# Seven of eight chunk pairs by Strassen's form, statistics by ScalarE's squares, and T1/T4 products one stage later, in a two-layer interaction kernel

## The chip, the cores and the metric

The kernel runs on one core of a Trainium2 chip. The metric is the device time of one execution in microseconds; a time quoted here is the median of the runs of its kernel, three to twenty-three of them. All profiles shown are of runs in the fast state, at a granted TensorE clock of 0.99 to 1.00.

## The reference

Two layers. Each forms all products of the fields of its input with the 32 fields of x, contracts them with a weight matrix, and normalizes each output channel over all rows and embedding places. Half of the first layer's output feeds the second.

```
def _batchnorm(h, gamma, beta):          # h: [4096, 128, 16]
    mean, var over (rows, embedding)
    return (h - mean) * rsqrt(var + 1e-5) * gamma + beta
def _cin_layer(out, x, W, b, gamma, beta):
    h = einsum('rne,rfe->rnfe', out, x).reshape(r, -1, e)
    h = einsum('rce,oc->roe', h, W) + b
    return _batchnorm(h, gamma, beta)
h1 = _cin_layer(x, x, W1, ...)           # W1: [128, 1024]
out, direct1 = h1[:, :64], h1[:, 64:]
direct2 = _cin_layer(out, x, W2, ...)    # W2: [128, 2048]
return concatenate([direct1, direct2], axis=1).sum(axis=-1)
```

## The kernel before

The change is in the second layer. It goes through 64 chunks; a chunk holds two groups of 512 sites. In each chunk there are four stages (i = 3, 0, 1, 2), and in each stage two slices q of 128 contraction rows. One stage and one slice make a product of 2 x 2 blocks: two halves of 64 output channels, two operands. Done plainly it needs eight products of 128x64 weights with 128x512 data; in Strassen's form (Winograd's variant) it needs seven, with sums of weight blocks S1 to S4, made once, and sums of data T1 to T4. T3 comes out of VectorE's multiply directly, because the difference of the x fields is multiplied; GpSimd adds T2 = T3 + B11 and then in one instruction T1 and T4 (B22 - T2 and B21 - T2). Eight such "pairs" of stage and slice make a chunk. Before the change six of them are Strassen's (stages S1, S2, S3) and two plain (stage P, i = 3), so 6 x 7 + 2 x 8 = 58 products.

A product has 64 output columns and uses one half of TensorE's columns ("low" or "high" by its place in the PSUM bank); two products on different halves run together (in the trace of the kernel before they start 0.01 us apart, and the next two 0.43 us later). Products are named x0 to x7 by the accumulator that they add to; a bank holds two accumulators (bank x62 has x6 low and x2 high). In the changed code `x1`, `x32`, `x67` and `x54` issue a stage's products for these accumulators; `x54` are those of T1 and T4.

```
STAGES = (3, 0, 1, 2); PLAIN = 3
psum  = tile_pool(name="psum", bufs=6, PSUM); factors = tile_pool(bufs=2, PSUM)
z2pool = tile_pool(name="z2pool", bufs=3); tpool = tile_pool(name="tpool", bufs=2)

def strassen(sums_, i, z, stop):
    t = tpool.tile([P, 3, 2, T], FP, tag="t", name="t")
    b11, t3, b22, b21 = (z[:, k] for k in range(4))
    t2, t1, t4 = (t[:, k] for k in range(3))
    queue("pool", lambda: nc.gpsimd.tensor_tensor(t2, t3, b11, ALU.add))
    twice = t2.unsqueeze(1).to_broadcast([P, 2, 2, T])
    queue("pool", lambda: nc.gpsimd.tensor_tensor(t[:, 1:3], z[:, 2:4], twice, ALU.subtract))
    sums_.matmul(1, w[0][0], b11[:, 0], stop)
    sums_.matmul(0, w[1][0], b11[:, 1], stop)
    for (x, kx, bx), (y, ky, by) in (
        ((3, 7, b22), (2, 2, b21)), ((6, 5, t2), (7, 6, t3)), ((5, 4, t1), (4, 3, t4)),
    ):
        for q in range(2): ...        # one product on each half

# combine(c): nine steps, spread over the next chunk:
#   both (ScalarE, from bank x11), both + x11, e = both + x62, u2, u3 = u2 + x57, ...,
#   statistics of e (VectorE), sums over embedding (VectorE)
```

VectorE writes z by two multiplies a stage, the factors f come from ScalarE, and `combine` finishes the chunk before, between them. The program gives every engine its instructions in a fixed order. A tile of t, of which there are two buffers, takes the buffer of the tile two before it, and its first writer waits for the last reader of that whole tile: in the changed kernel S2's T2 sum starts 0.09 us after the end of P's last T4 product, which had read another part of it (the timelines in the result).

## Time and profile before

| | before |
|---|---|
| time | 2125.4 us |
| second layer | from 501 us to the end |
| products in it | 64 x 58, two passes each of 0.429 us |
| once-a-chunk interval, mean of the last 62 | 25.02 us |

The lines, and the busy time of each engine in the second layer, are in the prediction. The once-a-chunk interval is that between the starts of the ScalarE instruction `both<-x`; I leave out the first interval, as the pipeline fills there.

### The profile page before, as it was taken

To read this page: it belongs to the slowest core of one execution; us is meant where nothing else is said; L and a number is where in the kernel's file an instruction comes from. 1 tells how busy PE (TensorE), PEld (TensorE's weight loads), DVE (VectorE), ACT (ScalarE), POOL (GpSimd) and SP (SyncE) were. 2 spreads that over 40 slices of the span, in tenths; PEclk is the share of its full clock that TensorE was granted. 3 is DMA by queue.
4 is the path that set the end of the run, shared out by engine and by line. 5 is a ranking of instruction groups with operands and counts; after the bars stand their busy time and mean duration, and the time that the engine had idled before them with its cause. 6 is when DMAs were issued, how large, how long until landed. Compare 5 with 4: busy or idle time off the path is not lost.

```text
span 2125.5 us, 23438 instructions
## 1 busy us (share of the span) xinstructions
PE 2095.5 (99%) x8732; PEld 736.3 (35%) x8732; DVE 1911.2 (90%) x1461; ACT 856.5 (40%) x1236; POOL 1330.4 (63%) x391
## 2 busy tenths in 40 slices
PE   9999999999999999999999999999999999999996
PEld 3444444443333333333333333333333333333332
DVE  7988879887999999899999998999999989999996
ACT  3555555553443333333333333333333333433332
POOL 0000000003888888878888888788888888888885
PEclk9999999999999999999999999999999999999998
DMA  9999999997677777776668777766677777676751
GB/s 348 359 341 345 326 342 365 364 334 201 159 168 189 181 183 172 172 174 159 165 162 198 173 172 173 174 161 166 162 179 171 171 174 172 164 166 161 171 137 40
DMA packets 112019, 440.65 MB, mean 207 GB/s; under 512 B 13088, under 2 KB 13088, under 8 KB 103456
## 3 DMA queue, kind: packets, MB, share of 16 engines
q1 hardware_dynamic: 105456, 418.43, 72.9%
q10 hardware_dynamic: 6448, 20.72, 2.6%
q8 instruction: 68, 1.11, 0.2%
q14 instruction: 47, 0.39, 0.1%
HBM read 417.07 MB, written 22.02 MB: 207 GB/s over the span
## 4 chain that ended last, share of the span: by engine, by line
PE 85%; POOL 9%; DVE 3%; issue 2%; ACT 1%; DMA 0%; DVEq 0%; SPq 0%; POOLq 0%
PE x L521 62%; PE ps L378 21%; POOL t L540 6%; POOL t L537 3%; PE ps L340 2%; DVE zz L491 2%; ACT both L483 1%; DMA b<-in_xb 0%; DVE e L486 0%; DVE zz L496 0%; PE running L404 0%; DVE x L188 0%; DVE z L347 0%; DVE d L687 0%; ACT u L483 0%
## 5 line engine op out<-in xcount | busy, mean ns | idle before, releaser
L521 PE MATMUL x<-zz,w_sb 128*64 128x512 f32 x2560 | 966.0, 592 | 0.0
L521 PE MATMUL x<-zz,s_sb 128*64 128x512 f32 x2048 | 932.4, 592 | 0.7 <-PE running L404 0.7
L537 POOL TENSOR_TENSOR t<-zz 128x1024 f32<-128x1024 f32 x192 | 456.6, 2378 | 753.0 <-DVE zz L491 753.0
L540 POOL TENSOR_TENSOR t<-zz,t 128x2048 f32<-128x2048 f32 x192 | 876.0, 4562 | 15.0
L521 PE MATMUL x<-t,s_sb 128*64 128x512 f32 x1536 | 696.1, 594 | 6.8 <-POOL t L540 6.4
L483 ACT ACTIVATE f<-a,keep 128x512 f32<-128x512 f32 x512 | 398.2, 778 | 629.9 <-DVE zz L491 623.8
L491 DVE TENSOR_TENSOR zz<-f,b 128x2048 f32<-128x2048 f32 x255 | 580.5, 2277 | 0.0
L491 DVE TENSOR_TENSOR zz<-f,bx 128x2048 f32<-128x2048 f32 x255 | 580.5, 2276 | 0.0
L378 PE MATMUL ps<-z,w_sb 128*128 128x512 f32 x1024 | 450.4, 597 | 2.2 <-DVE z L347 2.2
L521 PEld LDWEIGHTS x<-zz,s_sb 128*64 128x64 f32 x2048 | 280.5, 137 | 366.1 <-issue 350.3
L521 PEld LDWEIGHTS x<-t,s_sb 128*64 128x64 f32 x1536 | 205.2, 137 | 456.7 <-issue 396.7
L521 PE MATMUL x<-t,w_sb 128*64 128x512 f32 x768 | 363.2, 595 | 0.0
L347 DVE TENSOR_TENSOR z<-a,b 128x2048 f32<-128x2048 f32 (+1 forms) x129 | 293.6, 2277 | 62.8 <-DMA b<-in_xb 35.9
L521 PEld LDWEIGHTS x<-zz,w_sb 128*64 128x64 f32 x2560 | 300.6, 137 | 109.6 <-issue 106.1
L378 PEld LDWEIGHTS ps<-z,w_sb 128*128 128x128 f32 x1024 | 192.2, 190 | 258.0 <-issue 246.0
L521 PE MATMUL x<-zz,neg_sb 128*64 128x512 f32 x512 | 240.6, 592 | 0.0
L305 ACT ACTIVATE e<-ps,bn_sb 128x512 f32<-128x512 f32 x127 | 87.2, 687 | 240.9 <-PE ps L378 206.7
L486 DVE TENSOR_TENSOR both<-both,x 128x512 f32<-128x512 f32 x64 | 44.0, 688 | 130.2 <-ACT both L483 130.2
L483 ACT ACTIVATE u<-e,bn_sb 64x512 f32<-64x512 f32 x64 | 46.2, 722 | 193.6 <-DVE e L486 193.6
L521 PEld LDWEIGHTS x<-zz,neg_sb 128*64 128x64 f32 x512 | 70.1, 137 | 145.9 <-issue 145.9
L521 PEld LDWEIGHTS x<-t,w_sb 128*64 128x64 f32 x768 | 100.0, 137 | 0.0
L483 ACT ACTIVATE both<-x 64x512 f32<-64x512 f32 x64 | 38.0, 593 | 138.7 <-PE x L521 138.7
(74 smaller groups left out, 894.4 us busy)
## 6 DMA issues: line engine op xcount, KB each, us to landing
a<-h SPq DMA_DIRECT2D x256, 512.0 KB, 5.4
a<-in_xa SPq DMA_DIRECT2D x128, 512.0 KB, 6.0
b<-in_xb SPq DMA_DIRECT2D x128, 512.0 KB, 7.0
b<-in_xb SPq DMA_DIRECT2D x64, 1024.0 KB, 7.1
bx<-in_xb SPq DMA_DIRECT2D x64, 512.0 KB, 6.1
bx<-x SPq DMA_DIRECT2D x64, 512.0 KB, 7.9
h<-kept ACTq DMA_DIRECT2D x64, 256.0 KB, 5.8
r<-in_xr SPq DMA_DIRECT2D x16, 512.0 KB, 8.2
```

The source lines that it names most:

```text
L305: nc.scalar.activation(e, ps, AF.Identity, bias=b1)
L340: nc.tensor.matmul(pss[t + k], w1_sb[rows, 4 + t % GROUP // 4, :], zr[rows, :], start=not ended, stop=ended)
L347: return nc.vector.tensor_tensor(z[:, k], a.rearrange("p (a t) -> p a t", a=2)[:, k].unsqueeze(2).to_broadcast([P, n, 2, T]), b.rearrange( ...
L378: nc.tensor.matmul(pss[t], w1_sb[:, m, :], z[:, m // 2, m % 2, :], start=(t == m == 0), stop=(t > 0 and m == 3))
L483: return queue("act", lambda: nc.scalar.activation(to, source, AF.Identity, **scale_bias))
L486: return dve(lambda: nc.vector.tensor_tensor(to, x, y, ALU.add))
L491: dve(lambda: nc.vector.tensor_tensor(z, a, b.rearrange("p (k q) t -> p k q t", k=2), ALU.mult))
L521: queue("pe", lambda: nc.tensor.matmul(self.of[x], w, b, start=start, stop=stop))
L537: queue("pool", lambda: nc.gpsimd.tensor_tensor(t2, t3, b11, ALU.add))
L540: queue("pool", lambda: nc.gpsimd.tensor_tensor(t[:, 1:3], z[:, 2:4], twice, ALU.subtract))
```

## The change

Three things, meant to take work off TensorE and VectorE. First, one slice of the plain stage goes to Strassen's form too: 57 products a chunk; since that is odd, the half on which a chunk begins alternates, so that two chunks fill both halves evenly. Second, VectorE's statistics of the second layer go to ScalarE as squares with an accumulated sum (except in the last two chunks), and the difference of two x tiles becomes a reduction with a single operand, after ScalarE has negated one of them. Third, the products of T1 and T4, which wait for GpSimd longest (in the kernel before, TensorE's products and weight loads wait 65.8 us in all for T1/T4 sums and 0.4 us for T2 sums), are issued one stage later.

```diff
+            self.qs = (1,) if i == PLAIN else (0, 1)
+            t = tpool.tile([P, 3, 2, T], FP, tag="t", name="t")
+            ...
+            q = slice(self.qs[0], 2)
+            n = len(self.qs)
+            queue("pool", lambda: nc.gpsimd.tensor_tensor(t[:, 0, q], z[:, 1, q], z[:, 0, q], ALU.add))
+            twice = t[:, 0, q].unsqueeze(1).to_broadcast([P, 2, n, T])
+            queue("pool", lambda: nc.gpsimd.tensor_tensor(t[:, 1:3, q], z[:, 2:4, q], twice, ALU.subtract))
 ...
-        dve(lambda: stats_x.add(e[:, 0]))
-        dve(lambda: stats_y.add(e[:, 1]))
+        if c < MOST:
+            queue("act", lambda: add_square(c, 0, e))
 ...
-                ordinary(sums_, z)
+                stage.ordinary(low_first, 0)
+                stage.x1(low_first)
             else:
-                strassen(sums_, i, z, k == 3)
+                stage.x1(not low_first)
+            stage.x32(not low_first)
+            if k > 0:
+                waiting.x54(not low_first)
+            stage.x67(not low_first)
+            waiting = stage
+            if k == 3:
+                stage.x54(not low_first)
```

(Cut: the statistics' totals on ScalarE, the difference, and the order of PSUM banks, x11 now first.)

More of the change, by code (lines that the diff above doesn't have):

```diff
@@ L175, in load_bx, with negate @@
         return bx
-    xs = {}
+    xs = xpool.tile([P, 2, 2 * T], FP, tag="x", name="xs")
+    xd = xpool.tile([P, 2 * T], FP, tag="xd", name="xd")
     def load_x(g, k):
-        x = xs[k] = xpool.tile([P, 2 * T], FP, tag=f"x{k}", name="x")
         at = xb.offset + ((2 * DIFF * g + 1) * WRAP + 2 * k) * T
-        nc.sync.dma_start(x, bass.AP(xb.tensor, at, [[2 * WRAP * T, DIFF], [4 * T, 8], [1, 2 * T]]))
+        nc.sync.dma_start(xs[:, k], bass.AP(xb.tensor, at, [[2 * WRAP * T, DIFF], [4 * T, 8], [1, 2 * T]]))
+    def negate(part):
+        x = xs[:, 0, part * T : (part + 1) * T]
+        return nc.scalar.activation(x, x, AF.Identity, scale=-1.0)
     def difference(part):
-        cols = slice(part * T // 2, (part + 1) * T // 2)
-        return nc.vector.tensor_tensor(xs[1][:, cols], xs[1][:, cols], xs[0][:, cols], ALU.subtract)
+        to = slice(part * T // 2, (part + 1) * T // 2)
+        return nc.vector.tensor_reduce(xd[:, to], xs[:, :, to].rearrange("p k t -> p t k"), AX.X, ALU.add)
     def store_difference(g):
-        return nc.scalar.dma_start(diffs[g], xs[1])
+        return nc.scalar.dma_start(diffs[g], xd)
     EARLY = [(12, lambda: load_x(0, 1)), (16, lambda: load_x(0, 0)), (41, lambda: store_difference(0))]
+    EARLY += [(30 + 2 * k, lambda k=k: negate(k)) for k in range(2)]
     EARLY += [(34 + 2 * k, lambda k=k: difference(k)) for k in range(4)]
@@ L314, in finish @@
                 return ps
-            evict_direct(ed[to, :], ps)
+            done = evict_direct(ed[to, :], ps)
             if half == 1:
                 sum_direct(c)
+            return done
         def evict_direct(ed, ps):
-            nc.scalar.activation(ed, ps[KEEP:, :], AF.Identity, bias=b1[KEEP:])
+            return nc.scalar.activation(ed, ps[KEEP:, :], AF.Identity, bias=b1[KEEP:])
         def sum_direct(c):
@@ L383, in tile_cin @@
             if t > 0:
-                finish(t - 1)
+                evicted = finish(t - 1)
             if t == 20:
                 combine_weights()
-            with tc.issue_after(loads[-1].ins), tc.issue_after(product.ins):
+            if t == 0:
+                continue
+            with tc.issue_after(loads[-1].ins), tc.issue_after(product.ins), tc.issue_after(evicted.ins):
                 if t == 12:
@@ L453, in tile_cin @@
     d2 = sums.tile([P, 2, NC, RT], FP, tag="sum2", name="d2")
-    groups_of = -(-(NC - LAST) // SG) + 1
-    groups2 = const.tile([P, 2, groups_of, 3], FP, tag="groups2", name="groups2")
-    stats_x, stats_y = Stats("x", NC), Stats("y", NC, groups2[:, 0])
-    for g, size in enumerate(stats_x.sizes):
-        nc.vector.memset(groups2[:, 1, g, 0:1], size / LAST)
-    def swap_group(g):
+    MOST = NC - 2
+    groups_x = const.tile([P, 5, 3], FP, tag="groupsx", name="groups_x")
+    groups2 = const.tile([P, 2, 5, 3], FP, tag="groups2", name="groups2")
@@ new lines, in tile_cin @@
+    for group in (groups_x, groups2[:, 0]):
+        nc.vector.memset(group[:, 0, 0:1], float(MOST * T))
+    groups_of = (groups_x, groups2[:, 0])
+    squares = const.tile([P, 2, MOST], FP, tag="squares", name="squares")
+    totals = const.tile([P, 2, 4], FP, tag="totals", name="totals")
+    first = const.tile([P, 2, 6], FP, tag="first", name="first")
+    center = const.tile([P, 2, 1], FP, tag="center", name="center")
+    moments = const.tile([P, 2, 4], FP, tag="moments", name="moments")
@@ new lines, in tile_cin, with find_center, add_square, sum_up @@
+    unread = cpool.tile([P, T], FP, tag="unread", name="unread")
+    def find_center():
+        for s in range(2):
+            done = nc.vector.bn_aggr(moments[:, s, 0:2], first[:, s])
+        return done
+    def add_square(c, s, e):
+        return nc.scalar.activation(
+            unread, e[:, s], AF.Square, bias=center[:, s], accum_out=squares[:, s, c : c + 1]
+        )
+    def sum_up(to, source, scale=1.0):
+        return nc.scalar.activation(
+            unread[:, : source.shape[-1]], source, AF.Identity, scale=scale, accum_out=to
+        )
@@ new lines, in add_total, with most @@
+    def add_total(g, s):
+        d = d2[:, s, 16 * g : min(16 * (g + 1), MOST)].rearrange("p c r -> p (c r)")
+        return sum_up(totals[:, s, g : g + 1], d)
+    def most(s):
+        n = MOST * T
+        mean, total, off, square = (moments[:, s, k : k + 1] for k in range(4))
+        group = groups_of[s][:, 0]
+        yield lambda: sum_up(total, totals[:, s], scale=1.0 / n)
+        yield lambda: sum_up(square, squares[:, s])
+        yield lambda: nc.scalar.activation(group[:, 1:2], total, AF.Identity)
+        yield lambda: nc.scalar.activation(off, total, AF.Square, bias=center[:, s])
+        yield lambda: nc.scalar.activation(group[:, 2:3], off, AF.Identity, scale=float(-n), bias=square)
@@ L462, in swap_group @@
+    def swap_group(which):
         for x, y in ((low, high), (high, low)):
-            last = nc.scalar.activation(groups2[x, 1, g, 1:3], stats_x.groups[y, g, 1:3], AF.Identity)
+            last = nc.scalar.activation(groups2[x, 1, which], groups_x[y, which], AF.Identity)
         return last
@@ L467, in tile_cin @@
     nc.vector.tensor_copy(b2_swapped[low], b2[high])
-    idle, swaps = [lambda: sum_direct(NC - 1)], []
+    idle = [lambda: sum_direct(NC - 1)]
     lasts = {}
@@ L510, in __init__ @@
         def __init__(self):
-            banks = [psum.tile([P, T], FP, tag="ps", name=name) for name in ("x62", "x34", "x57", "x11")]
-            x62, x34, x57, x11 = self.banks = banks
+            banks = [psum.tile([P, T], FP, tag="ps", name=name) for name in ("x11", "x62", "x34", "x57")]
+            x11, x62, x34, x57 = self.banks = banks
             self.of = {
@@ L521, in matmul @@
             queue("pe", lambda: nc.tensor.matmul(self.of[x], w, b, start=start, stop=stop))
-    def ordinary(sums_, z):
-        for k in (0, 2, 1, 3):
-            q = k % 2
-            z1, z2 = z[:, 0 if k < 2 else 3, q], z[:, 2 if k < 2 else 1, q]
-            a11, a21, a12, a22, s1, s2, s3, s4 = weights(PLAIN, q)
-            sums_.matmul(3, s4 if k < 2 else neg_sb[:, 0, q], z2)
-            sums_.matmul(2, a11 if k < 2 else a12, z1)
-            sums_.matmul(5, s1 if k < 2 else neg_sb[:, 1, q], z2)
-            sums_.matmul(4, a21 if k < 2 else a22, z1)
@@ L533, in strassen, with __init__, two, ordinary @@
-    def strassen(sums_, i, z, stop):
-        t = tpool.tile([P, 3, 2, T], FP, tag="t", name="t")
-        b11, t3, b22, b21 = (z[:, k] for k in range(4))
-        t2, t1, t4 = (t[:, k] for k in range(3))
-        queue("pool", lambda: nc.gpsimd.tensor_tensor(t2, t3, b11, ALU.add))
-        twice = t2.unsqueeze(1).to_broadcast([P, 2, 2, T])
-        queue("pool", lambda: nc.gpsimd.tensor_tensor(t[:, 1:3], z[:, 2:4], twice, ALU.subtract))
-        w = [weights(i, q) for q in range(2)]
-        sums_.matmul(1, w[0][0], b11[:, 0], stop)
-        sums_.matmul(0, w[1][0], b11[:, 1], stop)
-        for (x, kx, bx), (y, ky, by) in (
-            ((3, 7, b22), (2, 2, b21)),
-            ((6, 5, t2), (7, 6, t3)),
-            ((5, 4, t1), (4, 3, t4)),
-        ):
-            for q in range(2):
-                sums_.matmul(x, w[q][kx], bx[:, q], stop and q == 1)
-                sums_.matmul(y, w[q][ky], by[:, q], stop and q == 1)
+    class Stage:
+        def __init__(self, sums_, i, z, last):
+            self.matmul, self.stop = sums_.matmul, last
+            self.w = [weights(i, q) for q in range(2)]
+            self.b11, self.t3, self.b22, self.b21 = (z[:, k] for k in range(4))
+            self.qs = (1,) if i == PLAIN else (0, 1)
+            t = tpool.tile([P, 3, 2, T], FP, tag="t", name="t")
+            self.t2, self.t1, self.t4 = (t[:, k] for k in range(3))
+            q = slice(self.qs[0], 2)
[3 more added lines that the diff above has]
+            queue("pool", lambda: nc.gpsimd.tensor_tensor(t[:, 1:3, q], z[:, 2:4, q], twice, ALU.subtract))
+        def two(self, low_first, *halves):
+            for x, w, b, stop in halves if low_first else halves[::-1]:
+                self.matmul(x, w, b, self.stop and stop)
+        def ordinary(self, low_first, q):
+            a11, a21, a12, a22, s1, s2, s3, s4 = self.w[q]
+            minus_s3, minus_a21 = neg_sb[:, 0, q], neg_sb[:, 1, q]
+            for x, u, y, v in ((3, s4, 2, a11), (5, s1, 4, a21)):
+                self.two(low_first, (x, u, self.b22[:, q], False), (y, v, self.b11[:, q], False))
+            for x, u, y, v in ((3, minus_s3, 2, a12), (5, minus_a21, 4, a22)):
+                self.two(low_first, (x, u, self.t3[:, q], False), (y, v, self.b21[:, q], False))
+        def x1(self, low_first):
+            halves = [(x, self.w[q][0], self.b11[:, q], True) for x, q in zip((1, 0), self.qs)]
+            if len(self.qs) == 1 and not low_first:
+                halves[0] = (0, *halves[0][1:])
+            self.two(low_first, *halves)
+        def products(self, low_first, x, kx, bx, y, ky, by):
+            for q in self.qs:
+                stop = q == 1
+                self.two(low_first, (x, self.w[q][kx], bx[:, q], stop), (y, self.w[q][ky], by[:, q], stop))
+        def x32(self, low_first):
+            self.products(low_first, 3, 7, self.b22, 2, 2, self.b21)
+        def x67(self, low_first):
+            self.products(low_first, 6, 5, self.t2, 7, 6, self.t3)
+        def x54(self, low_first):
+            self.products(low_first, 5, 4, self.t1, 4, 3, self.t4)
@@ L553, in combine @@
     def combine(c, sums_):
-        x62, x34, x57, x11 = sums_.banks
+        x11, x62, x34, x57 = sums_.banks
         both = cpool.tile([P, T], FP, tag="both", name="both")
@@ L580, in combine @@
         yield
-        dve(lambda: stats_x.add(e[:, 0]))
-        dve(lambda: stats_y.add(e[:, 1]))
-        if stats_x.ended():
-            g = stats_x.group
-            ends = [stats_x.close(), stats_y.close()]
-            if c < NC - 1:
-                swaps.append(g)
-                idle[:0] = ends
-            else:
-                dve(ends[0])
-                queue("act", lambda: swap_group(g))
-                dve(ends[1])
-        elif swaps and not idle:
-            g = swaps.pop()
-            queue("act", lambda: swap_group(g))
+        if c == 0:
+            for s in range(2):
+                dve(lambda: nc.vector.bn_stats(first[:, s], e[:, s]))
+            dve(find_center)
+            for s in range(2):
+                act(center[:, s], moments[:, s, 0:1], scale=-1.0)
+        if c < MOST:
+            queue("act", lambda: add_square(c, 0, e))
+        else:
+            at = slice(1 + 2 * (c - MOST), 3 + 2 * (c - MOST))
+            for s in range(2):
+                stats = groups_of[s][:, at].rearrange("p a b -> p (a b)")
+                dve(lambda: nc.vector.bn_stats(stats, e[:, s]))
+                if s == 0:
+                    queue("act", lambda: swap_group(at))
         yield
@@ L601, in combine @@
         )
+        if c < MOST:
+            queue("act", lambda: add_square(c, 1, e))
+        if c % 16 == 15 or c == MOST - 1:
+            sums_left.extend(lambda s=s: add_total(c // 16, s) for s in range(2))
+        if c == MOST - 1:
+            for s in range(2):
+                sums_left.extend(most(s))
+            sums_left.append(lambda: swap_group(slice(0, 1)))
         yield
+    sums_left = []
     steps = iter(())
@@ L619, in tile_cin @@
             if c % DIFF == 4:
+                for k in range(2):
+                    queue("act", lambda: negate(k))
                 idle += [lambda k=k: difference(k) for k in range(4)]
@@ L645, in tile_cin @@
                 step()
-            if k == 2:
-                step()
             if k < 3:
@@ L651, in tile_cin @@
                 step(2)
+            if k == 2:
+                step()
+            for _ in range(min(len(sums_left), 4 if c == NC - 1 else 1)):
+                queue("act", sums_left.pop(0))
             if k == 1:
                 step()
+            stage = Stage(sums_, i, z, k == 3)
+            low_first = c % 2 == 0
             if i == PLAIN:
-                ordinary(sums_, z)
-            else:
-                strassen(sums_, i, z, k == 3)
+                stage.ordinary(low_first, 0)
+                stage.x1(low_first)
+            else:
+                stage.x1(not low_first)
[6 more added lines that the diff above has]
+                stage.x54(not low_first)
             if c == k == 2:
@@ L666, in tile_cin @@
         steps = combine(c, sums_)
+    assert not sums_left
     step(8)
```

## The prediction

> **What bounds the kernel now.** I read the page's engine table first, then its groups, then a window over the second layer, then the timeline of one chunk there.
>
> ```profile
> PE 2095.5 (99%) x8732; PEld 736.3 (35%) x8732; DVE 1911.2 (90%) x1461; ACT 856.5 (40%) x1236; POOL 1330.4 (63%) x391
> ```
>
> The first layer ends near 500 us and is not touched beyond a few small operations. All the rest is 64 equal chunks, each of four stages (first the plain one, P, then the Strassen stages S1, S2, S3). The window over the second layer:
>
> ```profile
> 509.00:2104.00 1595.00, 1588.18 (x7377) 524.28 (x7375) 1464.19 (x1038) 598.61 (x837) 1324.68 (x384) 1.00 0.70 167
> ```
>
> TensorE is busy 1588 of 1595 us, VectorE 1464, ScalarE 599, GpSimd 1325. So TensorE is the bound, but GpSimd is at 83% here, not at the 63% that the page gives for the whole span. How they meet is in the timeline of GpSimd and then of TensorE, around the end of one chunk (start, duration, instruction):
>
> ```profile
> 1199.90 4.55 POOL L540 TENSOR_TENSOR t<-zz,t 128x2048 f32<-128x2048 f32 x1
> 1208.37 2.37 POOL L537 TENSOR_TENSOR t<-zz 128x1024 f32<-128x1024 f32 x1 [3.92 <-DVE zz L491]
> 1210.82 4.56 POOL L540 TENSOR_TENSOR t<-zz,t 128x2048 f32<-128x2048 f32 x1
> 1215.34 2.38 POOL L537 TENSOR_TENSOR t<-zz 128x1024 f32<-128x1024 f32 x1
> ```
>
> ```profile
> 1204.01 0.59 PE L521 MATMUL x<-t,s_sb 128*64 128x512 f32 x1
> 1204.01 0.59 PE L521 MATMUL x<-zz,s_sb 128*64 128x512 f32 x1
> 1204.50 0.64 PE L521 MATMUL x<-t,s_sb 128*64 128x512 f32 x1
> 1204.51 0.64 PE L521 MATMUL x<-t,w_sb 128*64 128x512 f32 x1
> 1204.98 0.59 PE L521 MATMUL x<-t,s_sb 128*64 128x512 f32 x1
> 1204.99 0.59 PE L521 MATMUL x<-t,w_sb 128*64 128x512 f32 x1
> ```
>
> Three readings. (1) Two instructions, one on each column half, start together every 0.43 us; a product has two such passes (58 products a chunk, 64 chunks, 7424 instructions), so a pair of products takes 0.858 us and a product counts for u = 0.429 us: 58 u = 24.89 us a chunk. (2) GpSimd takes 1215.34 - 1208.37 = 6.97 us for one Strassen stage (2.45 from T2's start to T1/T4's, 4.52 to the next T2), thus 20.9 us a chunk, and then stands idle 3.92 us because the plain stage gives it nothing. (3) The last T1/T4 sum of the chunk ends at 1204.45 and the products that read it start at 1204.50, 0.06 us behind the beat: TensorE only just waits for GpSimd at the end of each chunk.
>
> ```profile
> L483 ACT ACTIVATE both<-x x64: 593/593/595, 524.6 to 2101.6; 64x512 f32<-64x512 f32 x64
> ```
>
> This row of the tile view gives the measured period: it happens once a chunk, so (2101.6 - 524.6)/63 = 25.03 us, of which 24.89 are products and 0.14 waits.
>
> [...]the two halves start 0.01 us apart. [...]the trace has 4562 ns for the subtraction of 2048 and 2378 for 1024, so a line of 0.19 us + 2.13 ns per element. [...]GpSimd's 2048-element sums stay between 4530 and 4593 ns in all 192[...].[...]
>
> **The change part by part.**
>
> TensorE: half of the plain stage goes from 8 products to 7, so a chunk has 57. Alternating halves across two chunks keep both halves equally loaded. 57 u = 24.46 us, 0.43 less per chunk, 27.5 us over 64. That is the whole possible gain, apart from the 0.14 of waits.
>
> GpSimd: the plain stage gets sums on one half: by the line above 1.28 us for 512 elements and 2.38 for 1024, with the gaps seen (0.08 between the two, -0.04 to the next stage) 3.70 us. A chunk becomes 20.93 + 3.70 = 24.6 us. That alone is above the 24.46 of TensorE: GpSimd's idle 3.92 us is all used.
>
> VectorE: two statistics passes of 0.68 and 0.67 us a chunk leave, 1.35 us. The differences grow from 0.42 to some 0.67 us each (512 inputs in place of 256), but there are only 16 of them, most of them in a place where VectorE waits for TensorE. VectorE gets some 2 us of slack a chunk.
>
> ScalarE: two squares[...] plus the read of the sum a chunk; with 599 of 1595 us busy and the factors needed one multiply ahead, I expect nothing from it. The statistics' totals go into the last two chunks beside products. In the tail two aggregations (0.25 and 0.22 us) go: -0.4 us. The first layer: two negations and a longer wait of early work, beside products: 0.
>
> Order of T1 and T4: this is the step that decides. The tile of sums t has two buffers, and in the built program of the kernel before, the first sum of a stage waits for the last T4 product of two stages earlier, that is, for the whole tile, not for the part that it overwrites. With the new order, in units u from the start of the chunk: P is 8 + 1 + 2 + 2 = 13; S1 is 2 + 4, then the two T1/T4 products of P as numbers 20 and 21, then 4; S2 is 2 + 4 + 4 + 4; S3 is 2 + 4 + 4 + 4, then at once its own four T1/T4 products, since nothing is left to put them behind. So:
> - Sums of S2 reuse P's buffer and cannot begin before product 21 ends. Products pair up on the halves, so 21 runs beside 22 and ends at 22 u.
> - From there GpSimd does S2 and S3 without a break: 2.46 + 4.52 + 2.46 + 4.56 = 14.00 us.
> - Then TensorE does the four products of S3 and the first 22 u of the next chunk: 1.77 us (1204.50 to 1206.27 in the trace, with the start after a wait) + 9.44.
> - Latencies: 0.16 us from the beat to the recorded end of a product (0.59 - 0.43), an estimated 0.09 from that end to GpSimd's start (it takes 0.08 from its own T2's end to T1/T4), 0.05 from GpSimd's end to the product.
> Sum: 14.00 + 1.77 + 9.44 + 0.16 + 0.09 + 0.05 = 25.51 us. It is a closed loop, one turn a chunk, and longer than TensorE's 24.46, GpSimd's 24.6 and today's 25.03. VectorE fits inside: after each chunk's start S1's inputs are ready near 0.8 us, S2's near 7 and S3's near 12.7, and GpSimd wants them at 1.9, 9.7 and 16.7.
>
> The first chunk ends about where it does now (some 530 us: there GpSimd's three Strassen stages follow each other in both). So 63 x (25.51 - 25.03) = +30 us, -0.4 in the tail: 2125.4 + 30 = 2155 us. I take 2152, a little towards the better rivals.
>
> **Rivals.** (a) TensorE stays the bound: 24.46 plus 0.05 of waits, 63 x 0.52 = 33 us less, 2092. For it: TensorE is 99% busy, one product in 58 goes. Against it: GpSimd's own 24.6. (b) GpSimd's work is the bound without the buffer's wait: 24.64, 25 us less, 2101. For it: the delayed products were meant to give it slack, and the end of S1 to the start of S2 costs only about 0.8 us in my loop. It would be right if the sums of S2 could start before product 21 ended; the waits of the program before speak against it. (c) The loop holds but 21 ends at 21 u, because the halves run staggered: 25.08, 2128. (d) Something further on VectorE or ScalarE, such as a square that delays a factor: each tenth of a microsecond a chunk is 6 us; 0.2 make 2168.
>
> **Range and chances.** The loop is built of durations that hardly vary in the trace, so I put most weight near 2155; its soft parts are the pairing (c) and the latency, which can only bring it down by 0.4 us a chunk, and (d). Range 2122 to 2169. Faster by over 2% would be below 2083, under rival (a), which is already the most that the removed products can give: 0.02. Slower by over 2% is above 2168: 0.11.
>
> **What would show it.** In the changed kernel: TensorE waits for the T1/T4 sums about once a chunk by 0.6 to 1.0 us, at the fifty-fourth product; GpSimd has one idle gap a chunk of some 0.8 us, before the T2 sum of S2, ended by TensorE; the once-a-chunk row has a period of 25.5; the small sums take 1.28 and 2.38 us; VectorE idles 2 us or more a chunk. I am wrong if GpSimd's gap before S2 is missing (then b), or if TensorE never waits (then a), or if GpSimd waits for VectorE before S1 or S2 (then d).

## The result

The changed kernel takes 2153.6 us (2151.8 to 2154.8, four runs) against 2125.7 us. The ratio is 1.013, 95% interval 1.0113 to 1.0148: 1.3% slower, which counts as the same at a threshold of 2%. A ratio is the mean time of one kernel's fast runs over that of the other's in the same rounds, so it is not quite the ratio of the medians quoted; the kernel before was timed again in each set of rounds, with medians of 2124.5 to 2125.7 us. The result is correct.

The engine table of the page, and the window over the second layer (engines in the order of the table), both of the changed kernel:

```profile
PE 2104.0 (98%) x8604; PEld 736.7 (34%) x8604; DVE 1846.4 (86%) x1317; ACT 969.0 (45%) x1522; POOL 1561.7 (73%) x519
```

```profile
509.00:2130.00 1621.00, 1594.96 (x7240) 523.95 (x7238) 1398.07 (x906) 709.62 (x1121) 1549.33 (x510) 1.00 0.71 164
```

TensorE has 128 records fewer (64 products of two passes), and yet its busy time is longer: a product that runs alone, while its partner on the other half waits, counts in full (1.02 us for number 53 below). VectorE is relieved as intended (1398 us busy in a longer stretch), ScalarE takes 110 us more. GpSimd is at 1549 of 1621 us, 96%. Most of the missing 4% is in its timeline over one chunk (start, duration, instruction, idle time before it and what ended it):

```profile
1202.00 2.38 POOL L584 TENSOR_TENSOR t<-zz 128x1024 f32<-128x1024 f32 x1 [0.82 <-PE x L570]
1204.46 4.56 POOL L587 TENSOR_TENSOR t<-zz,t 128x2048 f32<-128x2048 f32 x1
1208.98 2.35 POOL L584 TENSOR_TENSOR t<-zz 128x1024 f32<-128x1024 f32 x1
1211.41 4.55 POOL L587 TENSOR_TENSOR t<-zz,t 128x2048 f32<-128x2048 f32 x1
1215.92 1.28 POOL L584 TENSOR_TENSOR t<-zz 128x512 f32<-128x512 f32 x1
1217.28 2.37 POOL L587 TENSOR_TENSOR t<-zz,t 128x1024 f32<-128x1024 f32 x1
1219.62 2.38 POOL L584 TENSOR_TENSOR t<-zz 128x1024 f32<-128x1024 f32 x1
1222.08 4.57 POOL L587 TENSOR_TENSOR t<-zz,t 128x2048 f32<-128x2048 f32 x1
1227.47 2.37 POOL L584 TENSOR_TENSOR t<-zz 128x1024 f32<-128x1024 f32 x1 [0.82 <-PE x L570]
```

The first two lines are S2, the next two S3, then the small sums of P, then S1, then S2 of the next chunk. Before, GpSimd waited once a chunk for VectorE, ahead of S1; now it runs without a gap except ahead of S2, where TensorE ends the wait. Its idle time is 0.82 us, and the turn from 1202.00 to 1227.47 is 25.47 us. What it waits for is in TensorE's timeline of the same place:

```profile
1200.89 0.59 PE L570 MATMUL x<-t,w_sb 128*64 128x512 f32 x1
1200.90 0.59 PE L570 MATMUL x<-t,s_sb 128*64 128x512 f32 x1
1201.32 0.59 PE L570 MATMUL x<-t,w_sb 128*64 128x512 f32 x1
1201.33 0.59 PE L570 MATMUL x<-t,s_sb 128*64 128x512 f32 x1
```

The product with w_sb is T4 of P, number 21; beside it runs number 22, x6 of S1 (the one with s_sb). Number 21 ends at 1201.32 + 0.59 = 1201.91, and GpSimd starts at 1202.00. The other end of the loop, where S3's T1/T4 sum is ready at 1211.41 + 4.55 = 1215.96:

```profile
1214.63 1.02 PE L570 MATMUL x<-zz,s_sb 128*64 128x512 f32 x2
1216.01 0.64 PE L570 MATMUL x<-t,s_sb 128*64 128x512 f32 x1 [0.37 <-POOL t L587]
1216.02 0.64 PE L570 MATMUL x<-t,w_sb 128*64 128x512 f32 x1
...
1217.78 0.59 PE L570 MATMUL x<-zz,s_sb 128*64 128x512 f32 x1
1217.79 0.59 PE L570 MATMUL x<-zz,w_sb 128*64 128x512 f32 x1
```

Number 53 runs alone on its half for two passes from 1214.63; number 54, the first with T1 or T4, could have started beside it and starts 1.38 us later. There the loss arises: 1.38 us, less the 0.43 us that number 53 counts for in any case, and 0.05 us more for the start after a wait (1216.01 to 1216.49, in place of 0.43 us) are 1.00 us, of the 1.02 us by which the period of 25.48 us (below) exceeds 57 u. Only 0.37 us of it is idle time of the whole engine. The table of waits sums both sides (waiter <- releaser: us in total, times, longest):

```profile
POOL t L584 <- PE x L570: 51.7, 63, 0.9
...
PE x L570 <- POOL t L587: 26.2, 64, 2.7
```

Both wait for each other in every chunk: the mark of a closed loop, in which neither engine is full.

```profile
L531 ACT ACTIVATE both<-x x64: 594/594/596, 519.3 to 2127.8; 64x512 f32<-64x512 f32 x64
```

The mean of the last 62 intervals of this row is 25.48 us, against 25.02 before, so 62 x 0.46 = 28.5 us longer. The second of these instructions starts 2.3 us earlier than before, and the span goes on 1.3 us longer after the last: 28.5 - 2.3 + 1.3 = 27.5, and the spans differ by 27.6.

### The profile page after: what moved, and what is told of

The parts are those of the page before. It is cut to its first block, busy times and chain, and to the rows that moved or that the text cites. A ratio compares the mean times of both kernels' runs of the same rounds, so it can differ in the third digit from the quotient of the medians.

```text
span 2153.1 us, 23463 instructions
## 1 busy us (share of the span) xinstructions
PE 2104.0 (98%) x8604; PEld 736.7 (34%) x8604; DVE 1846.4 (86%) x1317; ACT 969.0 (45%) x1522; POOL 1561.7 (73%) x519
## 4 chain that ended last, share of the span: by engine, by line
PE 44%; POOL 29%; DVE 14%; issue 12%; ACT 0%; DMA 0%; POOLq 0%; DVEq 0%; SPq 0%
PE x L570 22%; PE ps L384 21%; POOL t L587 20%; POOL t L584 9%; DVE zz L539 9%; DVE e L534 2%; DVE d L667 2%; PE ps L346 2%; ACT both L531 0%; DMA b<-in_xb 0%; DVE zz L544 0%; POOLq L847 0%; DVE xd L192 0%; PE running L412 0%; DVE u L534 0%
## 5 line engine op out<-in xcount | busy, mean ns | idle before, releaser
L587 POOL TENSOR_TENSOR t<-zz,t 128x2048 f32<-128x2048 f32 (+1 forms) x256 | 1029.0, 4020 | 20.1
L584 POOL TENSOR_TENSOR t<-zz 128x1024 f32<-128x1024 f32 (+1 forms) x256 | 537.8, 2101 | 545.1 <-DMA a<-h 493.0
L570 PE MATMUL x<-zz,w_sb 128*64 128x512 f32 x2304 | 915.0, 592 | 0.0
L570 PE MATMUL x<-t,s_sb 128*64 128x512 f32 x1792 | 824.9, 594 | 12.1 <-POOL t L587 12.1
L570 PE MATMUL x<-t,w_sb 128*64 128x512 f32 x896 | 429.6, 596 | 14.2 <-POOL t L587 14.1
L570 PEld LDWEIGHTS x<-zz,w_sb 128*64 128x64 f32 x2304 | 282.6, 137 | 347.2 <-issue 346.4
L570 PEld LDWEIGHTS x<-t,s_sb 128*64 128x64 f32 x1792 | 239.9, 137 | 274.5 <-issue 224.1
L570 PEld LDWEIGHTS x<-t,w_sb 128*64 128x64 f32 x896 | 117.3, 137 | 154.7 <-issue 110.8
L570 PE MATMUL x<-zz,neg_sb 128*64 128x512 f32 x256 | 120.3, 592 | 0.0
L485 ACT ACTIVATE unread<-e,center 128x512 f32<-128x512 f32 x124 | 89.6, 722 | 26.3 <-DVE e L534 24.5
```

The lines of the kernel that those rows point to most:

```text
L485: return nc.scalar.activation(unread, e[:, s], AF.Square, bias=center[:, s], accum_out=squares[:, s, c : c + 1])
L570: queue("pe", lambda: nc.tensor.matmul(self.of[x], w, b, start=start, stop=stop))
L584: queue("pool", lambda: nc.gpsimd.tensor_tensor(t[:, 0, q], z[:, 1, q], z[:, 0, q], ALU.add))
L587: queue("pool", lambda: nc.gpsimd.tensor_tensor(t[:, 1:3, q], z[:, 2:4, q], twice, ALU.subtract))
```

## The experiments

Theory L is the prediction's: the sums of S2 wait for product 21 through the shared buffer of t, and the loop sets the period. Rival W: the period comes from the work itself or from other waits. Rival D: the delay of T1/T4 is needed, and the rest is at fault. All kernels below gave correct results. "Period" is the mean of the last 62 once-a-chunk intervals.

| run | median us | ratio to before | period us |
|---|---|---|---|
| before | 2125.7 | | 25.02 |
| after | 2153.6 | 1.0130 | 25.48 |
| own_buffer | 2100.0 | 0.9877 | 24.60 |
| p_t14_first | 2099.2 | 0.9875 | 24.59 |
| p_t14_last | 2269.2 | 1.0673 | 27.28 |
| own_stage | 2122.1 | 0.9984 | 25.00 |
| delay_alone | 2117.8 | 0.9967 | 24.89 |
| rest_alone | 2124.2 | 0.9995 | 25.01 |
| t2_vector_two | 2113.9 | 0.9947 | 24.83 |
| t2_vector_reduce | 2099.8 | 0.9879 | 24.60 |
| e_later_reduce | 2093.8 | 0.9853 | 24.51 |
| e_later_own | 2096.7 | 0.9867 | 24.58 |
| e_later_own_stage | 2099.0 | 0.9877 | 24.62 |

By the threshold of 2% all but p_t14_last (slower) count as the same. The 95% intervals of the ratios are at most 0.0035 wide, so differences of half a per cent are clear of noise; the smaller ones below rest on the periods in the traces.

**own_buffer: take away what makes S2 wait.** A third buffer for t was not run; P's sums need only half a tile.

```diff
+    ppool = ctx.enter_context(tc.tile_pool(name="ppool", bufs=1))
-            t = tpool.tile([P, 3, 2, T], FP, tag="t", name="t")
+            if i == PLAIN:
+                tp = ppool.tile([P, 3, 1, T], FP, tag="tp", name="tp")
+                ...
+            else:
+                t = tpool.tile([P, 3, 2, T], FP, tag="t", name="t")
 ...
```

> The changed kernel, but the plain stage's sums get a tile of their own (half size, one buffer), so that the sums of S2 no longer wait for product 21. Order of products and all other work unchanged. Theory L (the closed loop through the shared buffer sets the period of 25.48 us): GpSimd's idle gap of 0.82 us before S2 goes, its own work is then the bound, period 25.48 - 0.82 = 24.66 us, 63 x 0.82 = 52 us less, about 2102 us. Rival W (the 25.5 us come from the amount of work or from waits elsewhere: VectorE's factors, the squares, the halves not packing): no change, 2150 to 2155. If the time falls to about 2092, GpSimd's busy rows overstate it and TensorE is the bound.

Measured: 2100.0 us. GpSimd's timeline now, from P's sums to S2's:

```profile
1215.44 1.28 POOL L599 TENSOR_TENSOR tp<-zz 128x512 f32<-128x512 f32 x1
1216.79 2.38 POOL L602 TENSOR_TENSOR tp<-zz,tp 128x1024 f32<-128x1024 f32 x1
1219.14 2.38 POOL L599 TENSOR_TENSOR t<-zz 128x1024 f32<-128x1024 f32 x1
1221.60 4.57 POOL L602 TENSOR_TENSOR t<-zz,t 128x2048 f32<-128x2048 f32 x1
1226.13 2.37 POOL L599 TENSOR_TENSOR t<-zz 128x1024 f32<-128x1024 f32 x1
```

No gap is left; S2 starts when S1 is done. One buffer of 6 KB takes 53.6 us off, and the change that it was missing from turns from 1.3% slower into 1.2% faster. W falls.

**p_t14_first: the same without memory.** The two T1/T4 products of P go to the front of S1.

```diff
+                if k == 1:
+                    waiting.x54(not low_first)
                 stage.x1(not low_first)
             stage.x32(not low_first)
-            if k > 0:
+            if k > 1:
                 waiting.x54(not low_first)
```

> The changed kernel with the two T1/T4 products of the plain stage moved to the front of S1 (products 14 and 15 of the chunk instead of 20 and 21), buffers unchanged. Theory L: they end six products earlier, 2.6 us, which is more than the gap of 0.82 us, so the loop is slack and the time is as with the separate buffer, about 2102 us. Rival W: no change, 2150 to 2155, or slower if those products now wait for GpSimd.

Measured: 2099.2 us, as with the buffer, and the table of waits no longer has GpSimd waiting for TensorE. Two different edits that have only the end of the wait in common give the same time.

**p_t14_last: more of the suspected wait.** The same two products four places later.

```diff
-            if k > 0:
+            if k > 1:
                 waiting.x54(not low_first)
             stage.x67(not low_first)
+            if k == 1:
+                waiting.x54(not low_first)
```

> The changed kernel with the two T1/T4 products of the plain stage moved four products later, behind S1's x6/x7 (products 24 and 25 of the chunk). No work is added. Theory L: the loop grows by four products, 4 x 0.429 = 1.72 us a chunk, 63 x 1.72 = 108 us, about 2262 us, with GpSimd's gap before S2 at some 2.5 us. Rival W: no change, 2150 to 2155, since nothing but an order moves.

Measured: 2269.2 us, 7 us more than L said. GpSimd's wait ahead of S2:

```profile
1221.49 2.37 POOL L584 TENSOR_TENSOR t<-zz 128x1024 f32<-128x1024 f32 x1 [2.54 <-PE x L570]
```

The gap is 2.54 = 0.82 + 1.72 us, and 58 of the last 62 intervals are at 27.1 to 27.2 us, 1.70 above the changed kernel's. Most of the other 7 us are in the four that are left, of 28.8 to 28.9 us. (The first interval is 1.5 us longer than the changed kernel's.) At one of the four, in the window from 907 to 934 us, the mean clock granted to TensorE is 0.94, against 1.00 in the 27 us before and in the 27 us after; TensorE's timeline there:

```profile
907.73 1.11 PE L570 MATMUL x<-t,w_sb 128*64 128x512 f32 x1 [2.04 <-POOL t L587]
...
908.63 1.06 PE L570 MATMUL x<-t,w_sb 128*64 128x512 f32 x1
...
909.49 1.06 PE L570 MATMUL x<-t,w_sb 128*64 128x512 f32 x1
```

From the end of the wait on, four passes start 0.82 to 0.90 us apart, and 0.43 us apart otherwise: they take from 907.73 to 911.16, 3.43 us in place of 1.72, so 1.7 us are lost. Ahead of them a product runs alone on one half for 1.02 us, and then the whole engine is idle for 2.04 us. The table of waits has 132.9 us in 64 such waits of TensorE, 2.1 us on average, so only in four of the last 62 chunks did a wait of 2 us cost so much more than itself; what sets these four apart was not shown.

**own_stage: T1/T4 back in their own stage, all else kept.**

```diff
             stage.x32(not low_first)
-            if k > 0:
-                waiting.x54(not low_first)
             stage.x67(not low_first)
-            waiting = stage
-            if k == 3:
-                stage.x54(not low_first)
+            stage.x54(not low_first)
```

> The changed kernel with every stage's T1/T4 products back in their own stage, as before the change; 57 products, GpSimd's extra sums, squares and differences stay. Theory L: product 21 of the loop is now number 15, so the loop through the buffer is slack. What is left is the loop that bounds the kernel before: last x1/x0 product of a chunk, ScalarE, VectorE to S1's inputs, GpSimd's three Strassen stages, T1/T4 of S3 (49.9 us for two chunks there, up to 0.4 us less here), so a period of 24.75 to 24.95 us, or GpSimd's own 24.66: 2106 to 2120 us. Rival D (the delay helps and without it TensorE would wait more): above 2154.

Measured: 2122.1 us, 31.5 us faster than with the delay but 2 us above my range. So D falls: with 57 products and two buffers, the delay is what costs. But the gain of one product does not come either. GpSimd, ahead of S1:

```profile
1206.59 2.38 POOL L584 TENSOR_TENSOR t<-zz 128x1024 f32<-128x1024 f32 x1 [0.27 <-DVE zz L539]
```

It waits for VectorE's second multiply of S1 in nearly every chunk, by 0.35 us on average (19.9 us in 57 waits from 560 to 2060 us), most of the difference between 25.00 and GpSimd's own 24.60 us. The chain is a loop: TensorE's last x1/x0 product of a chunk, ScalarE (`both`), VectorE, GpSimd, TensorE. The kernel before has the same waits once a chunk: GpSimd's for VectorE and TensorE's for GpSimd are in the prediction's timelines, the other two in its table of waits:

```profile
ACT both L483 <- PE x L521: 138.7, 64, 10.9
DVE both L486 <- ACT both L483: 130.2, 64, 6.3
```

The median interval of own_stage is 24.95 us, the upper end of what I had given it. The rest of the miss is in six intervals of 25.5 to 25.8 us, two in each of the three stretches in which VectorE forms the differences, which stand in the middle of that loop.

**delay_alone and rest_alone: the parts of the change by themselves, with 58 products.** delay_alone is the kernel before with S1's and S2's T1/T4 products behind the next stage's x3/x2:

```diff
 ...
+        products(3, 7, b22, 2, 2, b21)
+        if later:
+            later.pop()()
+        products(6, 5, t2, 7, 6, t3)
+        later.append(lambda: products(5, 4, t1, 4, 3, t4))
+        if stop:
+            later.pop()()
```

> The kernel before with only the T1/T4 products of S1 and S2 one stage later (S3's stay); 58 products, statistics and differences as before. In theory L the delay does harm only where the plain stage has sums in the shared buffer; here it has none, the last x1/x0 products come four products earlier against the end of the chunk, and the small wait of 0.14 us a chunk goes: period 24.89 to 24.95, 2116 to 2121 us. Rival (the delay itself costs, by holding the buffers longer): 2130 or more.

Measured: 2117.8 us, with every interval after the first at 24.89 us, exactly 58 u. Alone, the delay does what it was made for: the period holds no wait of TensorE any more. rest_alone has P plain on both slices and T1/T4 in their own stage:

```diff
-            self.qs = (1,) if i == PLAIN else (0, 1)
+            self.qs = (0, 1)
+            if i == PLAIN:
+                return
...
-                stage.ordinary(low_first, 0)
-                stage.x1(low_first)
+                stage.ordinary(True, 0)
+                stage.ordinary(True, 1)
 ...
```

> The changed kernel with the plain stage ordinary on both halves (58 products, no sums of GpSimd for it) and T1/T4 in their own stage: what is left of the change is the squares on ScalarE, the differences by a reduction, and the order of the banks. Theory: the 1.35 us of VectorE's statistics lie outside the chain that bounds the kernel before (VectorE waits 2 us a chunk for TensorE anyway), so 2120 to 2130, the same. Rival (VectorE bounded the kernel before): 63 x up to 0.14 less, 2116.

Measured: 2124.2 us, the interval of the ratio is 0.9986 to 1.0003. The 1.35 us a chunk taken from VectorE bring nothing, though VectorE was at 92% in the second layer. So the delay by itself costs nothing, nor do the statistics and the difference, nor the step to 57 products together with these (own_stage; by itself it was not run); the loss is in delay and sums of P together, with two buffers.

**t2_vector_two and t2_vector_reduce: relieve GpSimd.** With own_buffer GpSimd is the bound. P's T2 goes to VectorE, once as an addition of two operands, once as a reduction over one (the lines that make `tp` are cut).

```diff
+                dve(lambda: nc.vector.tensor_tensor(tp[:, 0, 0], z[:, 1, 1], z[:, 0, 1], ALU.add))
or
+                dve(lambda: nc.vector.tensor_reduce(tp[:, 0, 0], z[:, 0:2, 1].rearrange("p k t -> p t k"), AX.X, ALU.add))
```

> The changed kernel with the separate tile of sums for the plain stage, and the T2 sum of the plain stage (512 elements) on VectorE, as an addition of two SBUF operands, in the place where VectorE waits for TensorE. Theory: GpSimd's work falls from 24.66 to 23.3 us a chunk and is no bound any more; what is left is TensorE's 24.46 us and the loop by way of VectorE, an estimated 24.55: 2153.6 - 63 x 0.93 = 2095 us, 1.4% faster than the kernel before. Rival: GpSimd is slowed by VectorE's two-operand addition and gives the gain back (its 2048 sums above 4.6 us): 2100 to 2110.

> As the run with the T2 sum of the plain stage on VectorE, but as a reduction over two elements of one operand (some 1.2 us in place of 0.7 us, no second SBUF operand). If two operands slow GpSimd down, this one is faster than the addition by up to 10 us and GpSimd's long sums are shorter; if they don't, both are 2095 within 3 us, as VectorE has the time.

Measured: 2113.9 and 2099.8 us; both miss 2095. The addition first (tile view: shortest, median, longest in ns; then a sum of GpSimd beside it):

```profile
L748 DVE TENSOR_TENSOR tp<-zz x64: 691/1264/1954, 499.8 to 2059.8; 128x512 f32<-128x512 f32 x64
```

```profile
1216.84 4.88 POOL L603 TENSOR_TENSOR t<-zz,t 128x2048 f32<-128x2048 f32 x1
```

In the first chunk, with no sum of GpSimd beside it, it takes 0.69 us. In 62 of the other 63 it starts beside S3's T2 sum and ends 0.55 to 0.59 us after that sum does, whether it began 0.1 or 1.4 us before the sum's end: its end goes with the sum's, not with its own start. So it takes 1.26 us in the median and up to 1.95, and the T1/T4 sum of GpSimd that follows takes 4.88 us here, in place of 4.56. Both engines lose where the two run side by side, which I had not seen in the kernel before (all its T1/T4 sums take 4.53 to 4.59 us). The reduction always takes 1.23 to 1.27 us, and GpSimd's long sums stay at 4.59 us or less. It is 14 us faster, so the expected sign with more than the expected size.

The reduction gains nothing over own_buffer, though GpSimd now has gaps. VectorE's timeline shows what took over:

```profile
1216.65 2.28 DVE L540 TENSOR_TENSOR zz<-f,b 128x2048 f32<-128x2048 f32 x1
1219.88 0.69 DVE L535 TENSOR_TENSOR e<-both,x 128x512 f32<-128x512 f32 x1 [0.94 <-PE x L571]
1220.48 2.29 DVE L540 TENSOR_TENSOR zz<-f,bx 128x2048 f32<-128x2048 f32 x1
```

Between the two multiplies of S1 stands the addition of the last chunk's e, which waits 0.94 us for TensorE, and GpSimd's S1 waits for the second multiply (1.38 us ahead of the S1 that starts at 1222.91). I had put this loop at 24.55 us; it is 24.60. In the profiled run a further 1.7 us are lost in the first chunk, at 530 us; the longest matmul with T1, T2 or T4 of a Strassen stage takes 1.06 us in this profile, and 0.64 us in own_buffer's. The profiled run took 2102.1 us and is the slowest of its four, so the median of 2099.8 need not contain this loss.

**e_later_reduce, e_later_own, e_later_own_stage: shorten the loop by way of VectorE.** The addition of e goes behind the second multiply, in three kernels; and P's first products are put in the order 3, 2, 3, 2, 5, 4, 5, 4.

```diff
-            if k in (1, 2, 3):
+            if k in (2, 3):
                 step()
             ...
-                if k == 1:
+                if k == 2:
                     step()
                 multiply(z[:, 1:3], f2, bx)
-            if k == 1:
+            if k in (1, 2):
                 step()
```

> The run with the plain stage's T2 as a reduction on VectorE, and on VectorE the first addition of x6+x2 (e), which waits 0.94 us for TensorE there, behind S1's second multiply in place of before it; the plain stage's first products reordered (3,2,3,2,5,4,5,4) so that x5/x7's bank, which that addition frees, is wanted later. Theory: its period of 24.58 us (24.52 and 24.66 by turns) is the loop VectorE, GpSimd's three Strassen stages, TensorE; S1's inputs come 1.5 us earlier, the loop is slack, and TensorE's 57 products are the bound: 24.46 to 24.50 us, 2092 to 2095. Rival: the period is set by something else (VectorE's own work, or some wait at TensorE): 2100 as before, or slower if u3 and what follows it come too late.

> The run with a separate tile for the plain stage's sums, all sums on GpSimd, with the same later addition and order of the first products. Theory: there GpSimd's own 24.6 us are the bound, its rows follow each other without a gap, so nothing changes: 2099 to 2102. Rival (the loop by way of VectorE is the bound there too): 2092 to 2095 as with the reduction.

> The run with T1/T4 in their own stage (2122 us, period 24.94), with the same later addition and order of the first products. Theory: there the loop VectorE, GpSimd, TensorE that bounds the kernel before is the bound, GpSimd waits for VectorE before S1; S1's inputs come 0.6 us earlier and the loop turns once in two chunks, 0.3 us a chunk: period 24.6 to 24.65, GpSimd's own, 2100 to 2106 us. Rival (the missing delay costs at TensorE): stays near 2122.

Measured: 2093.8, 2096.7 and 2099.0 us. The first is as expected: intervals of 24.51 us, 57 u = 24.46 plus 0.05; its window over the second layer:

```profile
509.00:2080.00 1571.00, 1561.02 (x7250) 653.69 (x7246) 1473.77 (x986) 701.81 (x1127) 1468.28 (x446) 1.00 0.74 169
```

TensorE is busy 99.4% again and GpSimd 93%, so the product that the change took away is gained at last: 1.5% faster than before. The second keeps own_buffer's period (24.58 against 24.60), so there GpSimd is the bound and not VectorE; it is 3.4 us faster than own_buffer and 2.4 us below my range. Of this, 62 x 0.02 = 1.2 us are in the period. In the profiles another 1.8 us lie before the second layer, which the edit does not touch: VectorE's first multiply there starts at 494.9 against 496.7 us, and in the thirteen profiles between 494.9 and 498.5. Some 1 us is also the rounds: the kernel before took 2124.5 us in these and 2125.5 in own_buffer's. The third takes own_stage from 25.00 to 24.62 us and just under the expected range: so what bounded own_stage is the loop by way of VectorE. For the kernel before the same follows from its waits and from delay_alone; the later addition was not tried with 58 products. The new order of P's products was always changed together with the addition, so no run tells their shares apart.

## Why the prediction was right

- **The bound before.** It said that TensorE is the bound and only just waits for GpSimd. That holds for the engine that is full (58 u of 25.02 us), but the 0.14 us are part of a loop through ScalarE, VectorE, GpSimd and TensorE, by the waits shown at own_stage, and GpSimd's idle 3.92 us, which the prediction put down to P alone, last until VectorE delivers. With delay_alone the loop is slack and exactly these 0.13 us go.
- **TensorE's term**, 57 u = 24.46 us: reached within 0.05 us by e_later_reduce. The halves do pack (a period of 24.51 us).
- **GpSimd's term**, 24.6 us: own_buffer runs it without a gap at 24.60 us. The small sums take 1.28 and 2.38 us, as read off the line through two sizes.
- **VectorE and ScalarE**: no gain and no loss, confirmed by rest_alone. The square takes 0.72 us and its read of the sum 0.19 us, as the tile of the squares has it.

```profile
L485 ACT ACTIVATE unread<-e,center 128x512 f32<-128x512 f32 x124 | 89.6, 722 | 26.3 <-DVE e L534 24.5
L485 ACT ACTIVATION_READ_ACCUMULATOR unread<-e,center 128x1 f32 x124 | 23.1, 186 | 0.0
```

- **The loop**, 25.51 us: measured 25.47, piece by piece 13.96 for GpSimd (14.00), 0.05, 1.77 for the four products (1.77), 9.60 for the next 22 u and the drain (9.44 + 0.16), 0.09 to GpSimd's start (0.09, an estimate then). The pairing of 21 with 22, which rival (c) denied, is seen in the trace. own_buffer and p_t14_first open the loop, p_t14_last lengthens it by what four products take. Rivals (a) and (b) describe kernels that exist: (b) is own_buffer, 2100 where 2101 was said, and (a) is e_later_reduce, with GpSimd relieved of P's T2, 2094 where 2092 was said; the buffer and VectorE's order kept the changed kernel from being either.
- **Smaller misses.** The first chunk was said to end where it does now; the second `both` instruction starts 2.3 us earlier, of which 1.7 us is its new place (four products further from the chunk's end). Of the other 0.6 us, 0.5 are the earlier start of the layer in this profile (VectorE's first multiply at 498.0 against 498.5 us). By its place alone the stretch after the last of these instructions would be 1.7 us longer; it is 1.3 us longer, so the 0.4 us said of the tail are there. The wait at product 54 was said to be 0.6 to 1.0 us; the trace shows 0.37 us of idle engine and 1.38 us of idle half. And I gave nothing for the reduction in place of a two-operand difference since GpSimd's long sums showed no loss (4.53 to 4.59 us); in t2_vector_two the long sum that follows beside a two-operand addition of VectorE took 4.88 us in place of 4.56, and in the trace before none of the 16 differences runs beside a sum of GpSimd, so its sums could not have shown a loss: the reading was empty, though little hangs on 16 instructions.

## What to carry to other kernels

When a consumer is delayed to hide a producer's latency, its buffer is held longer (here to product 21 in place of 15, and GpSimd waited 0.82 us a chunk for it); write down who frees the buffer of the next producer but one, and follow that wait once round the period. A loop in which two engines wait for each other once a period showed both almost full and neither as the bound here (TensorE 98% and GpSimd 96%); a small separate buffer, or an earlier place of the last reader, opened it (periods of 24.60 and 24.59 us in place of 25.48). When a bound is taken away, the next can be close: here GpSimd's work, the loop by way of VectorE and TensorE's work gave 24.60, 24.60 and 24.51 us, so the whole gain came only when both of the first were made shorter.
